# Half a slot later for the values, other places for projections, and SyncE in program order: a change to the attentions of a four-layer kernel

## The chip, the core and the metric

The kernel runs on one core of one Trainium2 chip. The core has five engines that run side by side, each with its own instruction queue: TensorE (PE: matrix products, with the loading of its weights shown as PEld), VectorE (DVE), ScalarE (ACT), GpSimd (POOL) and SyncE (SP), which here only issues transfers. Transfers are carried out by 16 DMA engines. An engine works its queue in order; an instruction that waits holds up everything behind it on its engine.

The metric is the device time of one execution in microseconds, the median of several runs.

## The reference

Four layers follow one another on activations of 8 batches x 256 tokens x 512 features, all in float32: a cross-attention with injected context, a recurrent layer (time mix and channel mix), a transformer decoder block, and a non-local block. The change is in the third, the decoder block, cut here to its attentions:

```python
ln_out = layernorm(hidden_states, ln1_s, ln1_b)
q, k, v = jnp.split(ln_out @ w_qkv + b_qkv, 3, axis=-1)
ctx = merge_heads(attention(split_heads(q), split_heads(k), split_heads(v), ltor_mask))
x = hidden_states + ctx @ w_ao + b_ao

ln_out = layernorm(x, ln2_s, ln2_b)
q = ln_out @ w_q + b_q
k, v = jnp.split(encoder_states @ w_kv + b_kv, 2, axis=-1)
ctx = merge_heads(attention(split_heads(q), split_heads(k), split_heads(v), cross_mask))
x = x + ctx @ w_co + b_co
```

with 16 heads of 32, 256 queries and 256 keys for each batch, and

```python
def attention(q, k, v, mask):
    scores = jnp.einsum('bhqd,bhkd->bhqk', q, k) / jnp.sqrt(jnp.float32(HD))
    scores = scores * mask - 10000.0 * (1.0 - mask)
    probs = jax.nn.softmax(scores, axis=-1)
    return jnp.einsum('bhqk,bhkd->bhqd', probs, v)
```

So there is a self-attention and then a cross-attention, each over 8 batches. The keys and values of the cross-attention come from `encoder_states`, an input of the program.

## The kernel before

One method, `plan`, lays out layer three's attentions together with the recurrent layer before them. The list `runs` has 16 items: the 8 batches of the self-attention (prefix `a_`) and then the 8 of the cross-attention (`c_`). Every item has `CT` = 4 slots, one for each group of 4 heads (128 features), so there are 64 slots, numbered n, which follow the slots of the recurrent layer.

What a slot holds is set in the loop at the end of `plan`. In slot n, in this order:

- `scores(n+1)`: 16 products on TensorE for the next slot's 4 heads (L1127), into PSUM.
- For each of two streams (two heads each): `masked` (VectorE, L1139 and L1142: scale and mask, add, running minimum), `exps` (ScalarE, L1151), `divided` of the stream before (reciprocal on VectorE L1159, products on GpSimd L1161) and `turn` of the stream before that. `turn` transposes 32x32 blocks on VectorE (L1171, `dt`), writes the result to DRAM by a transfer that ScalarE issues (L1175), and reads it back in another order by 4 transfers that SyncE issues (L1177, `pt`). Each of these reads waits for the write, and the write for the transpose. `pt` has two buffers for each of the two streams.
- `fill.until(A0 + n + 0.95)`: the projections and other steps whose place lies in this slot.
- `values(n-1)`: 16 products on TensorE with `pt` of the slot before (L1190), emptied by ScalarE into `cx` (L1194).
- `fill.until(A0 + n + 0.99)`.

The steps that `fill` holds are put in by a table of offsets: a step with offset `at` for item i runs at the place `A0 + CT * i + at`, that is, `at` slots after the item's first slot. The steps of an item are: `at_fetch` (the item's input, `axi`, L1010), `at_inputs` (for the cross-attention the transposed encoder states, `enc`, L1019, one buffer, and the mask `mk`, L1021), `at_norm` and `at_normed` (layer norm, statistics on VectorE; `away` is L1035), `at_norm_T` (transposes on TensorE, L83, emptied by ScalarE), `at_q`, `at_k`, `at_v` (projections, two halves each, L817 and L881, emptied by ScalarE into `aq` L1055, `ak` L1066, `av` L1077), `at_residual` (the input once more, L1084), `at_biased` (GpSimd, L1089), `at_out` (output projection, two halves; its sum is L1095 on VectorE) and `at_store` (L1101). k and v of a cross-attention item read `enc`. Since offsets run from -7.5 to 6.8, the steps of three or four neighbouring items stand in one slot.

Before the change, the TensorE work of the four slots of an item (beside scores and values) is: v1, norm transposes, q1; then q0, out0; then k0, out1; then k1, v0; the values of the slot before stand at each slot's end. Here v1, q1 belong to the item that is running, out0 and out1 to the one before, the rest to the next.

TensorE's instructions keep the order of the program. On the other engines a planner places the instructions by estimated times, save those that are pinned by `pin` (`keep_in_program_order`): the steps of the softmax, the transfers of `turn` and the sums of `at_out` are pinned, the other transfers on SyncE are not. Weights are loaded through `spans`: each weight's entry gives from where to where it is in use, and a load goes out when one of five buffers comes free.

Of the kernel before, what the change touches and what calls it, by code (L numbers as in the profile page):

```python
# [16 lines left out]
P = 128  # L17
B, S, D = 8, 256, 512
# [603 lines left out]
class Middle:  # L622
# [62 lines left out]
    def plan(self):  # L685
        g, cp, wpool = self.g, self.cp, self.wpool
        nc, I = g.nc, g.I
# [19 lines left out]
        def new(tag, bufs=2):  # L707
            return wk.tile([P, CT, S], F32, tag=tag, name=tag, bufs=bufs)
# [4 lines left out]
        def mm(name):  # L713
            return ps.tile([P, 2, S], F32, tag="mm", name=name, bufs=bufs[0])
# [5 lines left out]
        t_ = {}  # L720
# [174 lines left out]
        def spread(b, ct, hf):  # L895

            v_ = t_["v", b]
            vb = vbs[b, ct, hf] = ps.tile([P, NG, 2, S], F32, tag="vb", name="vb", bufs=1)
            for j in range(2):
                for n in range(NG):  # L900
                    r = slice(32 * n, 32 * n + 32)
                    nc.tensor.matmul(  # L902
                        vb[:, n, j, 1:S], lhsT=esel[r, 2 * hf + j, :], rhs=v_[r, ct, 0 : S - 1],
                        start=True, stop=True,
                    )
# [30 lines left out]
        def gather(b, ct, hf):  # L936
            if hf == 0:
                yps[b, ct] = ps.tile([P, S], F32, tag="y", name="yp", bufs=1)
                if ct % 2 == 0:
                    t_["y", b, ct // 2] = wk.tile([P, 2, S], F32, tag="y", name="y", bufs=2)  # L940
            yp = yps[b, ct]
            rs2 = rss.pop((b, ct, hf))
            for j in range(2):
                for n in range(NG):
                    nc.tensor.matmul(
                        yp[32 * n : 32 * n + 32, :], lhsT=gsel[:, 2 * hf + j, :],
                        rhs=rs2[n // 2][:, 2 * (n % 2) + j, :],
                        start=(hf == 0 and j == 0), stop=(hf == 1 and j == 1),
                    )
            if hf == 1:  # L950
                nc.vector.tensor_tensor(
                    t_["y", b, ct // 2][:, ct % 2, :], yp, t_["hv", b][:, ct, :], ALU.add
                )
# [51 lines left out]
        pin = lambda ins: self.tc.keep_in_program_order(ins)  # L1005

        def at_fetch(i):
            pre, b = runs[i]
            x = t_["axi", i] = wk.tile([P, ST, D], F32, tag="xi", name="axi", bufs=1)
            nc.sync.dma_start(out=x, in_={"a_": g.x2, "c_": g.x3, "m_": g.x4}[pre][b])  # L1010

        def at_inputs(i):

            pre, b = runs[i]
            if pre == "a_":
                t_["mk", i], t_["mb", i] = t_["mask"]
                return
            enc = t_["src", i] = wk.tile([P, CT, S], F32, tag="kk", name="enc", bufs=1)
            nc.sync.dma_start(out=enc, in_=I["ctxT"][b].rearrange("(k p) s -> p k s", p=P))  # L1019
            mk = t_["mk", i] = wk.tile([P, ST, S], F32, tag="th", name="mk")  # L1020
            nc.sync.dma_start(out=mk, in_=I["mask_b"][b].rearrange("(t p) k -> p t k", p=P))  # L1021

        def at_mask(i):
            if runs[i][0] == "c_":
# [54 lines left out]
        def at_residual(i):  # L1079
            pre, b = runs[i]  # L1080
            x = t_["axo", i] = new(("hv", "csx")[i % 2], 1).rearrange("p c s -> p (c s)").rearrange(
                "p (t d) -> p t d", t=ST
            )
            nc.sync.dma_start(out=x, in_=(g.x2 if pre == "a_" else g.x3)[b])  # L1084

        def at_biased(i):
            pre, x = runs[i][0], t_["axo", i]
# [9 lines left out]
        def at_store(i):  # L1097
            pre, b = runs[i]
            to = g.x3 if pre == "a_" else g.x4
            to[b] = g.dram([P, ST, D], f"x{pre}{b}")  # L1100
            nc.sync.dma_start(out=to[b], in_=t_.pop(("axo", i)))  # L1101

        def at_load(W, src, col):
            t_[W, 0] = rows_of(g.weight(wpool, I[src], col, W))
# [17 lines left out]
        def scores(i, ct):  # L1122
            sps = t_["sp", i, ct] = [mm("sp") for _ in range(NH)]
            for qt in range(ST):
                for h in range(NH):
                    r = slice(h * HD, (h + 1) * HD)
                    nc.tensor.matmul(  # L1127
                        sps[h][:, qt, :], lhsT=t_["aq", i][r, ct, qt * P : (qt + 1) * P],
                        rhs=t_["ak", i][r, ct, :], start=True, stop=True,
                    )  # L1130
# [48 lines left out]
        def values(i, ct):  # L1179
            pts = [  # L1180
                t_.pop(("pt", i, ct, h2)).rearrange("p r (h t k q) -> p h k t r q", h=2, t=ST, k=ST)
                for h2 in range(2)
            ]
            if ct == 0:
                t_["cx", i] = wk.tile([P, CT, S], F32, tag="g", name="cx")
            cx = mm("cp")[:, 0, :]
            for kt in range(ST):
                for h in range(NH):
                    col = (NH * ct + h) * HD
                    nc.tensor.matmul(  # L1190
                        cx[h * HD : (h + 1) * HD, :], lhsT=t_["av", i][:, kt, col : col + HD],
                        rhs=pts[h // 2][:, h % 2, kt], start=(kt == 0), stop=(kt == ST - 1),
                    )
            nc.scalar.activation(t_["cx", i][:, ct, :], cx, AF.Identity, bias=g.pv(runs[i][0] + "bv", ct))  # L1194
# [31 lines left out]
        fill = self.fill = Filler()  # L1226
# [4 lines left out]
        A0 = 8 * B  # L1231
        for i in range(len(runs)):
            for at, fn, *args in (
                (-7.5, at_fetch), (-5.2, at_norm), (-4.3, at_normed), (-3.5, at_norm_T), (-3.6, at_inputs), (-1.6, at_mask),
                (-2.8, at_q, 0), (-1.8, at_k, 0), (-0.8, at_k, 1), (-0.3, at_v, 0), (0.2, at_v, 1), (0.7, at_q, 1),
                (2.8, at_residual), (4.8, at_biased), (5.7, at_out, 0), (6.7, at_out, 1), (6.8, at_store),
            ):
                fill.put(A0 + CT * i + at, lambda i=i, fn=fn, args=args: fn(i, *args))
        runs.append(("m_", 0))
# [14 lines left out]
        for pre, i, q, kv, o in (("a_", 0, "w_qkv", "w_qkv", "w_ao"), ("c_", B, "w_q", "w_kv", "w_co")):  # L1254
            c = D if q == kv else 0
            for W, lo, hi, src, col in (
                ("wq", -2.8, 0.7, q, 0), ("wk", -1.8, -0.8, kv, c), ("wv", -0.3, 0.2, kv, c + D), ("wo", 5.7, 6.7, o, 0)
            ):
                lo, hi = A0 + CT * i + lo, A0 + CT * (i + B - 1) + hi
                spans.append((lo, hi, lambda W=pre + W, src=src, col=col: at_load(W, src, col)))  # L1260
# [10 lines left out]
        def loop(psums):  # L1271
            every = [(b, ct, hf) for b in range(B) for ct in range(CT) for hf in range(2)]
            bufs[0] = 3
            fill.until(-0.001)
            spread(*every[0])
            for n, at in enumerate(every):
                states(*at)
                fill.until(n + 0.95)
                if n:
                    gather(*every[n - 1])  # L1280
                fill.until(n + 0.99)
                if n + 1 < len(every):
                    spread(*every[n + 1])
            gather(*every[-1])

            psums.close()
            self.ps = psums.enter_context(self.tc.tile_pool(name="atp", bufs=8, space=PSUM))
            bufs[0] = 8
            every = [(i, ct) for i in range(2 * B) for ct in range(CT)]
            stream = [(i, ct, h2) for i, ct in every for h2 in range(2)]  # L1290
            for n in range(-1, len(every)):
                if n + 1 < len(every):
                    scores(*every[n + 1])
                for k in (2 * n + 2, 2 * n + 3):
                    if k < len(stream):
                        masked(*stream[k])
                        exps(*stream[k])
                    if 0 < k <= len(stream):
                        divided(*stream[k - 1])
                    if 1 < k:  # L1300
                        turn(*stream[k - 2])
                fill.until(A0 + n + 0.95)
                if n > 0:
                    values(*every[n - 1])
                fill.until(A0 + n + 0.99)
            values(*every[-1])
            fill.until(999)
            psums.close()
            return t_["ln", 2 * B]
# [455 lines left out]
```

## Time and profile before

| what | us |
|---|---|
| median of 3 runs (lowest, highest) | 3442.02 (3440.96, 3446.04) |
| the profiled execution, its own time | 3442.65 |
| its span in the profile | 3440.9 |
| attention stretch, from the first scores to the start of the next part | 2172 to 2944 |
| start of the scores in first slots of the cross items (the first of them: 2569.25) | 2612.97, 2656.65, 2700.39, 2749.29, 2793.30, 2838.84, 2882.72 |
| of three self items | 2390.43, 2432.61, 2474.19, 2516.66 |

All times are from one execution, recorded by the hardware profiler; the span is the time from the first recorded instruction to the last. A row of the timeline gives the start, the duration, the engine, the line of the kernel, the operation with its output and inputs, the shape, and the number of instructions put together in the row; brackets at its end give the idle time of the engine just before it and what ended that. "ACTq" and "SPq" are the issuing of transfers on ScalarE and SyncE. The granted clock is that of TensorE: 1.0 is full speed.

### The profile page before, as it was taken

The numbers are of one execution on the slowest core, as the hardware profiler recorded it, in microseconds if no ns is written. First come the engines' busy times: TensorE is split into PE (matmuls) and PEld (weight loads), VectorE is DVE, ScalarE is ACT, GpSimd is POOL, SyncE is SP. The second block draws the span as 40 slices with busy tenths as digits, with TensorE's granted clock in tenths as the row PEclk, the third lists the DMA queues.
The fourth block names the chain that finished last, engine by engine and source line by source line (L and its number), as shares of the span: only waits on it lengthen the run. The fifth ranks groups of instructions, "written<-read, shape, count | busy, mean of one in ns | idle before, by whom it ended". The sixth has DMA issues, their size and how long they took to land. (4 is left out here: it accounts for less than half of the span.)

```text
span 3440.9 us, 68745 instructions
## 1 busy us (share of the span) xinstructions
PE 3195.8 (93%) x26496; PEld 2278.9 (66%) x26496; DVE 2407.8 (70%) x4175; ACT 1614.0 (47%) x4000; POOL 1664.5 (48%) x1776
## 2 busy tenths in 40 slices
PE   8999999999999988889999998799989897899999
PEld 6677776777777765656666665465555554689996
DVE  4667666667666663788788788667878777677771
ACT  3455555555555453233443333565656565323223
POOL 6533333333333222555665665343444444688872
PEclk9999999999999998989999999899999999899999
DMA  7666565655656533212233333466677666500002
GB/s 266 218 203 201 188 196 184 206 188 188 214 182 213 178 108 95 96 49 92 94 104 103 105 101 105 139 214 236 237 253 249 238 238 230 182 1 1 1 13 86
DMA packets 277365, 533.08 MB, mean 155 GB/s; under 512 B 25056, under 2 KB 153712, under 8 KB 272944
## 3 DMA queue, kind: packets, MB, share of 16 engines
q1 hardware_dynamic: 255712, 456.48, 41.2%
q10 hardware_dynamic: 20656, 70.39, 5.3%
q8 instruction: 211, 3.46, 0.4%
q0 software_dynamic: 672, 1.81, 0.2%
q14 instruction: 114, 0.93, 0.1%
HBM read 411.15 MB, written 117.44 MB: 154 GB/s over the span
## 5 line engine op out<-in xcount | busy, mean ns | idle before, releaser
L391 POOL TENSOR_SCALAR pe<-pe,rinv 128x512 f32<-128x512 f32 x256 | 177.0, 692 | 614.7 <-DVE rinv L390 604.9
L368 DVE TENSOR_REDUCE nmax<-sp 128x2 f32<-128x1024 f32 x256 | 309.0, 1217 | 183.6 <-PE sp L363 183.6
L933 POOL TENSOR_TENSOR rs<-a,r 128x1024 f32<-128x1024 f32 x128 | 303.1, 2383 | 252.4 <-DVE a L928 215.7
L1161 POOL TENSOR_SCALAR pe<-pe,rinv 128x256 f32<-128x256 f32 x512 | 235.3, 478 | 334.0 <-DVE rinv L1159 316.5
L1151 ACT ACTIVATE pe<-pe,nmax 128x256 f32<-128x256 f32 x512 | 254.6, 498 | 226.1 <-DVE nmax L1142 217.9
L377 ACT ACTIVATE pe<-sp,nmax 128x512 f32<-128x512 f32 x512 | 347.0, 683 | 11.2
L403 DVE STREAM_TRANSPOSE pt<-pe 128x1024 f32<-128x1024 f32 x256 | 312.8, 1231 | 24.2 <-POOL pe L391 15.3
L432 PE MATMUL av<-pt,vr 32*64 32x256 f32 x8192 | 264.6, 388 | 43.6 <-issue 34.9
L928 DVE TENSOR_TENSOR_SCAN a<-w,vb 128x1024 f32<-128x1024 f32 x128 | 287.4, 2276 | 4.8
L432 PEld LDWEIGHTS av<-pt,vr 32*64 32x64 f32 x8192 | 209.8, 135 | 110.8 <-issue 67.3
L363 PE MATMUL sp<-k,q 64*64 64x512 f32 x2048 | 265.8, 611 | 7.3 <-ACT pe L377 7.3
L373 ACT ACTIVATE nmax<-nmax 128x2 f32<-128x2 f32 x256 | 51.8, 202 | 399.9 <-DVE nmax L368 399.7
L303 PEld LDWEIGHTS gp<-t,ws 128*128 128x128 f32 x1512 | 184.8, 192 | 30.5 <-ACT pe L396 11.4
L303 PE MATMUL gp<-t,ws 128*128 128x128 f32 x1512 | 202.2, 277 | 1.8 <-POOL ws L289 1.4
L396 ACT ACTIVATE pe<-pe,rinv 128x512 f32<-128x512 f32 x256 | 182.5, 729 | 41.2 <-DVE rinv L390 41.2
L924 DVE TENSOR_TENSOR vb<-vb,k 128x1020 f32<-128x1020 f32 x128 | 157.2, 1228 | 4.4
L1171 DVE STREAM_TRANSPOSE dt<-pe 128x1024 f32<-128x1024 f32 x128 | 155.6, 1215 | 0.8 <-POOL pe L1161 0.7
L902 PE MATMUL vb<-v,mconstc 32*128 32x255 f32 x1024 | 98.9, 441 | 57.5 <-DVE a L928 57.2
L1443 ACT ACTIVATE h<-h,pvec 128x256 f32<-128x256 f32 x124 | 55.8, 500 | 200.7 <-DVE h L1412 162.5
L1190 PE MATMUL cp<-pt,av 128*32 128x256 f32 x1024 | 97.5, 411 | 55.4 <-DMA pt<-pt 50.1
L390 DVE RECIPROCAL rinv<-ssum 128x2 f32<-128x2 f32 x256 | 41.1, 161 | 146.8 <-ACT pe L377 146.8
L1139 DVE SCALAR_TENSOR_TENSOR sp<-sp,lconstb 128x512 f32<-128x512 f32 x128 | 88.1, 688 | 68.7 <-PE sp L1127 68.6
(310 smaller groups left out, 7623.0 us busy)
## 6 DMA issues: line engine op xcount, KB each, us to landing
pt<-dt ACTq DMA_DIRECT2D x128, 512.0 KB, 3.6
pt<-pt SPq DMA_DIRECT2D x512, 128.0 KB, 3.1
ws<-sqk SPq DMA_DIRECT2D x110, 512.0 KB, 5.0
wqk<-in_wqk_dram SPq DMA_DIRECT2D x70, 512.0 KB, 5.5
vr<-v SPq DMA_DIRECT2D x128, 256.0 KB, 4.7
ws<-sv SPq DMA_DIRECT2D x56, 512.0 KB, 4.8
wv<-in_wv_dram SPq DMA_DIRECT2D x36, 512.0 KB, 4.7
v<-vT SPq DMA_DIRECT2D x64, 256.0 KB, 2.5
```

Of the source, the lines that this page charges most:

```text
L303: nc.tensor.matmul(out[:, hf * P : (hf + 1) * P], lhsT=w[n](hf, k), rhs=a[n](hf, k), start=k == 0, stop=k == ST - 1,)
L363: nc.tensor.matmul(sp[a * 64 : (a + 1) * 64, h, :], lhsT=qs[b, 2 * un + a][r, ic], rhs=ks[b, 2 * un + a][r, :], start=True, stop=True,)
L368: nc.vector.tensor_reduce(nmax, sp, AX.X, ALU.max, negate=True)
L377: nc.scalar.activation(pe[:, h, :], sp[:, h, :], AF.Exp, bias=nmax[:, h : h + 1], scale=1.0 / DH ** 0.5, accum_out=ssum[:, h : h + 1],)
L391: nc.gpsimd.tensor_scalar(pe[:, 0, :], pe[:, 0, :], rinv[:, 0:1], 1.0, ALU.mult, ALU.mult)
L396: nc.scalar.mul(pe[:, 1, :], pe[:, 1, :], rinv[:, 1:2])
L403: nc.vector.transpose(pts[b, un][:, it], pe)
L432: nc.tensor.matmul(av[r][h * DH : (h + 1) * DH], lhsT=vr[rows_, kb, h * DH : (h + 1) * DH], rhs=pt[rows_, :, h, 32 * kb : 32 * kb + 32], s ...
L928: nc.vector.tensor_tensor_scan(a.rearrange("p n l -> p (n l)"), w4.rearrange("p n l -> p (n l)"), vb[:, 4 * n2 : 4 * n2 + 4, :].rearrange( ...
L933: nc.gpsimd.tensor_tensor(rs, a, rb, ALU.mult)
L1151: pin(nc.scalar.activation(pe[:, r, :], pe[:, r, :], AF.Exp, bias=nmax[:, r : r + 1], scale=-1.0, accum_out=ssum[:, r : r + 1],))
L1161: pin(nc.gpsimd.tensor_scalar(pe[:, r, :], pe[:, r, :], rinv[:, r : r + 1], 1.0, ALU.mult, ALU.mult))
```

## The change

Two things change places, and five transfers are pinned:

- `values` stood at the end of slot n and took slot n-1. It now stands in mid slot (after the steps with places below 0.45) and takes slot n-2. After the loop there are therefore two values instead of one.
- The offsets of seven steps change: `at_norm_T` from -3.5 to -3.4, `at_inputs` from -3.6 to -3.45, the first half of k from -1.8 to -2.3, `at_residual` from 2.8 to 3.3, the first half of the output projection from 5.7 to 6.2, `at_store` from 6.8 to 7.3; the spans of the weights of k and out follow. The TensorE work of an item's four slots is then: v1, values, norm transposes, q1; then q0, values, k0; then out0, values, out1; then k1, values, v0.
- SyncE's transfers for `axi`, `enc`, `mk`, the residual and the store are pinned to the order of the program, in which the reads of `turn` already were.

```diff
@@ at_fetch
-            nc.sync.dma_start(out=x, in_={"a_": g.x2, "c_": g.x3, "m_": g.x4}[pre][b])
+            pin(nc.sync.dma_start(out=x, in_={"a_": g.x2, "c_": g.x3, "m_": g.x4}[pre][b]))
@@ at_inputs
-            nc.sync.dma_start(out=enc, in_=I["ctxT"][b].rearrange("(k p) s -> p k s", p=P))
+            pin(nc.sync.dma_start(out=enc, in_=I["ctxT"][b].rearrange("(k p) s -> p k s", p=P)))
             mk = t_["mk", i] = wk.tile([P, ST, S], F32, tag="th", name="mk")
-            nc.sync.dma_start(out=mk, in_=I["mask_b"][b].rearrange("(t p) k -> p t k", p=P))
+            pin(nc.sync.dma_start(out=mk, in_=I["mask_b"][b].rearrange("(t p) k -> p t k", p=P)))
@@ at_residual
-            nc.sync.dma_start(out=x, in_=(g.x2 if pre == "a_" else g.x3)[b])
+            pin(nc.sync.dma_start(out=x, in_=(g.x2 if pre == "a_" else g.x3)[b]))
@@ at_store
-            nc.sync.dma_start(out=to[b], in_=t_.pop(("axo", i)))
+            pin(nc.sync.dma_start(out=to[b], in_=t_.pop(("axo", i))))
@@ the table of steps
-                (-7.5, at_fetch), (-5.2, at_norm), (-4.3, at_normed), (-3.5, at_norm_T), (-3.6, at_inputs), (-1.6, at_mask),
-                (-2.8, at_q, 0), (-1.8, at_k, 0), (-0.8, at_k, 1), (-0.3, at_v, 0), (0.2, at_v, 1), (0.7, at_q, 1),
-                (2.8, at_residual), (4.8, at_biased), (5.7, at_out, 0), (6.7, at_out, 1), (6.8, at_store),
+                (-7.5, at_fetch), (-5.2, at_norm), (-4.3, at_normed), (-3.4, at_norm_T), (-3.45, at_inputs), (-1.6, at_mask),
+                (-2.8, at_q, 0), (-2.3, at_k, 0), (-0.8, at_k, 1), (-0.3, at_v, 0), (0.2, at_v, 1), (0.7, at_q, 1),
+                (3.3, at_residual), (4.8, at_biased), (6.2, at_out, 0), (6.7, at_out, 1), (7.3, at_store),
@@ the spans of the weights
-                ("wq", -2.8, 0.7, q, 0), ("wk", -1.8, -0.8, kv, c), ("wv", -0.3, 0.2, kv, c + D), ("wo", 5.7, 6.7, o, 0)
+                ("wq", -2.8, 0.7, q, 0), ("wk", -2.3, -0.8, kv, c), ("wv", -0.3, 0.2, kv, c + D), ("wo", 6.2, 6.7, o, 0)
@@ the loop
-                fill.until(A0 + n + 0.95)
-                if n > 0:
-                    values(*every[n - 1])
+                fill.until(A0 + n + 0.45)
+                if n > 1:
+                    values(*every[n - 2])
                 fill.until(A0 + n + 0.99)
+            values(*every[-2])
             values(*every[-1])
             fill.until(999)
```

## Prediction, made before the changed kernel had run

> **What bounds the kernel now.** I read the totals, then the attention stretch by windows (where it starts and ends comes from the timeline of its `L1127`), then the list of waits there, then TensorE's and SyncE's timelines through one cross item, and last the places where the clock fell.
>
> ```profile
> PE 3195.8 (93%) x26496; PEld 2278.9 (66%) x26496; DVE 2407.8 (70%) x4175; ACT 1614.0 (47%) x4000; POOL 1664.5 (48%) x1776
> 2172.00:2390.00 218.00, 203.34 (x1066) 124.67 (x1068) 150.06 (x439) 130.98 (x389) 85.97 (x153) 0.95 0.61 211
> 2390.00:2517.00 127.00, 118.96 (x712) 71.94 (x709) 103.98 (x309) 85.05 (x261) 56.64 (x110) 1.00 0.70 239
> 2517.00:2569.00 52.00, 41.43 (x232) 25.29 (x224) 34.47 (x103) 26.79 (x84) 18.05 (x35) 0.93 0.79 273
> 2569.00:2883.00 314.00, 285.57 (x1642) 172.46 (x1636) 241.72 (x717) 196.78 (x600) 134.55 (x258) 0.96 0.69 240
> 2883.00:2944.00 61.00, 40.99 (x184) 18.12 (x182) 30.56 (x85) 21.08 (x68) 19.62 (x36) 0.78 0.72 246
> PE cp L1190 <- DMA pt<-pt: 50.1, 29, 6.9
> PE sp L1127 <- ACT aq L1055: 11.5, 10, 5.3
> DVE sp L1139 <- PE sp L1127: 128.7, 51, 8.7
> DVE away L1035 <- ACT ln_rstd L61: 24.8, 13, 3.3
> ```
>
> A window row gives its length, busy time of TensorE (with TensorE's weight loads next), VectorE, ScalarE and GpSimd, and the granted clock. TensorE sets the end: it is 93% busy, and in the 772 us from 2172 to 2944 it is busy 690.3. What the change can win is the other 81.7 us and the loss of clock. A wait row gives total, times, longest: the largest of TensorE's waits is that of the values for the transposed probabilities, 50.1 us. VectorE waits 128.7 us for scores, since TensorE issues them late.
>
> ```profile
> 2569.25 1.15 PE L1127 MATMUL sp<-ak,aq 32*128 32x256 f32 x16
> 2570.32 3.70 PE L881 MATMUL projs<-c_wv,enc 128*128 128x512 f32 x8
> 2573.86 1.04 PE L83 MATMUL ln_tp<-ident,axn 128*128 128x128 f32 x8
> 2574.73 3.62 PE L817 MATMUL proj<-ln,c_wq 128*128 128x256 f32 x16
> 2578.28 1.60 PE L1190 MATMUL cp<-pt,av 128*32 128x256 f32 x16
> 2580.92 1.15 PE L1127 MATMUL sp<-ak,aq 32*128 32x256 f32 x16 [1.04 <-ACT aq L1055]
> ...
> 2585.88 0.54 SPq L1019 DMA_DIRECT2D enc<-in_ctxT_dram  x1
> ...
> 2713.17 1.92 PE L1190 MATMUL cp<-pt,av 128*32 128x256 f32 x12 [2.96 <-DMA pt<-pt]
> 2715.02 2.09 PE L1127 MATMUL sp<-ak,aq 32*128 32x256 f32 x16
> ```
>
> Each row: start, length, what, and in brackets the idle time before it. T is the start of the scores ahead of v1 (first row). The last two rows show the other cost of a wait: after 2.96 us idle the scores take 2.09 instead of 1.15.
>
> **The change, part by part.** Steps by start-to-start: scores 1.07, v and output projections 3.53, q and k 3.55, norm transposes 0.87, values 1.0. An item is 4 scores, 4 values and 8 projections before and after: no work is added or removed, only order.
>
> *Values later.* Values of slot n-2 stand in mid slot. They need data read some 5 us (half a slot) longer ago, so the 50.1 us of waits should mostly go. Their result feeds only the output projections, which move 0.5 slot too. What the values covered is uncovered: between q1 and the scores that need it, ScalarE must empty q1. Before, these scores start at T+11.67 after values and 1.04 of wait. In the built order of ScalarE the two copies of q1 now stand behind all four norm copies and the probability transfer; I add 0.5 us (one such copy is 0.55). TensorE ends q1 at 1.07+3.53+1.0+0.87+3.55 = T+10.0 and starts scores at T+12.2: 2.2 us idle once per item. Bounds: 1.0 (ScalarE no later) to 4.3 (`aq` at its worst, 5.3, less the values' 1.0).
>
> *k0 earlier, out0 later.* k0 moves from the slot after the next scores to half a slot earlier. In self items its input is the normed tile, made in the slot before. In cross items it is `enc`, a transfer.
>
> *SyncE in order.* Pinned, `enc` goes out behind the 8 reads of its own slot and behind `axi`. It has one buffer, free only when v1 of the previous item has read it (T+4.6), but that is not what ends last: each probability read waits on SyncE for the write before it, which waits for VectorE's transposes (the last of the slot at T+9.4). Before, `enc` also stood behind those reads: issued at T+15.5 to T+17.7 over the items, median 15.7, and k0 could start 5.9 later (2585.88 to 2591.74). Now `axi` (0.5) stands ahead: 15.6 + 0.5 + 5.9 = T+22.0. TensorE asks for k0 at T+12.2 + 1.07 + 3.55 (q0) + 1.0 (values) = T+17.8. New wait: 4.2 us, in each of 7 cross items. Queued behind k0 on TensorE are the next scores, and VectorE waits for those. The residual's load no longer stops SyncE for 39.1 us at the first self item (its longest wait there); The store and the residual go half a slot later: the store's readers are in the next stage, and the residual keeps 1.5 slots (some 15 us) ahead of its bias on GpSimd, against a landing of some 5; nothing. The weights of k and out have their spans moved by half a slot and are loaded once for eight items; nothing. `mk` lands after `enc`, and the masks need it three slots later: nothing.
>
> The clock speaks against trading many small waits for one long one. Rows: half speed after idles of 2.96, 3.23, 4.89 and 6.06 us, 2.2 to 3.0 us lost each time; none after 2.62. [...]
>
> The sum, stretch by stretch:
> - A, 2172 to 2390, first five self items beside the end of the time mix: -6. Gone: the wait for ak of 4.4, pt of 2.8, cn of 2.1 and the half clock behind the first (about 1.9 on scores and k1): 11.2; added 4 exposures of aq at 2.2, less those that run behind other projections: 5. Bounds: -25 (idle 14.7 plus 5% clock of 218 us) and +4.
> - B, 2390 to 2517, three self items of 42.1. VectorE's floor is 34.7 busy + 2.0 for `away` (24.8/13) + 4.0 for scores = 40.7; TensorE's 12.2 + 27.5 = 39.7. 3 x 1.4 = 4.2, of which I take -3. Bounds -7 and 0.
> - C, 2517 to 2569, the first cross inputs: `enc` of that item is issued late whatever the order; k0 at T+26.4, then 21.8 of work and 2.6 of half clock = 50.8 against 52.6: -2. Bounds -6 and +4.
> - D, 2569 to 2883, seven cross items of 44.9. k0 at T+22.0; behind it k0, scores, out0, values, out1, scores, k1, values, v0 = 3.55+1.07+3.53+1.0+3.53+1.07+3.55+1.0+3.53 = 21.8; half clock 2.4. 46.2 per item: 7 x 1.3 = +9. Bounds: +33 (`enc` at T+24.4, the latest issue plus 0.5 + 6.2, and 3.4 of clock: 49.6) and -29 (no wait, VectorE's floor of 40.7).
> - E, 2883 to 2944, tail: 61 us of which TensorE is busy 41.0 at clock 0.78, waiting 4.9, 6.9, 4.1 for pt. Now scores of the last slot no longer stand behind the values that wait 4.9, so VectorE's last transpose comes some 7 us earlier (2922.1 - 2882.7 = 39.4, to about 32); the two last values and outputs follow it unchanged: -9 with the clock they regain. Bounds -12 and -2.
>
> -6 - 3 - 2 + 9 - 9 = -11. Outside 2172 to 2944 nothing moves but the earlier loads of the next stage's weights, off TensorE's path. The profiled execution took 3442.65 (span 3440.9 and 1.75 around it), 0.6 above the median 3442.02: 3442 - 11 = 3431.
>
> **Rivals.**
> - R1, `enc` comes in time. For: SyncE's reads now may run ahead, and a read lands in 3.1. Against: reads wait for writes that follow VectorE, not TensorE. Then cross items go like self items now, 42.1: D = -20, total -40: 3402.
> - R2, slower: `enc`, pinned behind reads, comes at T+24.4, and TensorE stands 6.6 us per cross item and then runs at half clock. For: the reads of an item with a late read put `enc` at T+17.7 already before; scores come 0.5 later and so do reads; the order now may not yield. Against: six of eight items were nearer 15.7. D = +33: +33 - 20 = +13: 3455. It decides from an `enc` ready at about T+23 (46.2 + 1.5 per item cancels the other gains).
> - R3, the waits only move: VectorE's chain, 34.7 us per item plus its stalls for `away` and scores, sets the item, and what pt loses aq gains. For: `aq` now is exposed in every item. Against: VectorE is idle 72 of the 314 us. Then A to D come to nothing and the tail gives 2: 3440.
> - That the change doesn't do what it says: the built order shows all moves; no chance given.
>
> **How the numbers follow.** What a measurement can't tell from no change is 0.2%, 6.9 us: 3435.1 to 3448.9. Forecast 0.45 (own range 3420 to 3444: faster 0.30, same 0.13, slower 0.02); R1 0.17 (faster); R2 0.26 (same 0.02, slower 0.24); R3 0.12 (faster 0.02, same 0.06, slower 0.04). Faster 0.49, same 0.21, slower 0.30. The range goes from R1's to R2's time, 3402 to 3455; half of each lies beyond, about 0.2 in all.
>
> **What would show it.** Waits of the values for pt under 15 us in all; scores after q1 waiting 1 to 3 us for aq in each item; k0 in cross items waiting about 4 us for `enc`, with the scores behind it near 2.09; items in 2569 to 2883 at about 46; the next stage 8 to 10 us sooner after T of the last cross item. Wrong if `enc` waits sum to under 10 us (R1) or over 40 (R2), or if VectorE's idle time in the cross stretch falls below 40 (R3).

## The result, and the profile after

The changed kernel takes 3484.38 us (median of 4, 3477.44 to 3488.63) against 3441.49 (median of 4): a ratio of 1.0123, 95% interval 1.0101 to 1.0146. It is slower by about 42 us, outside the range predicted (3402 to 3455). The profiled execution of it has a span of 3483.3 us, 42.4 more than before.

From the page and the windows of the changed kernel (the same five stretches as before, cut at the starts of the same instructions; length, busy times of PE, PEld, DVE, ACT, POOL, then the granted clock):

```profile
PE 3199.5 (92%) x26496; PEld 2279.9 (65%) x26496; DVE 2410.0 (69%) x4175; ACT 1619.3 (46%) x4006; POOL 1664.6 (48%) x1776
2170.00:2382.00 212.00, 200.68 (x1052) 120.92 (x1052) 150.08 (x445) 134.59 (x391) 85.02 (x151) 0.98 0.63 216
2382.00:2515.00 133.00, 121.28 (x701) 71.45 (x704) 105.40 (x310) 85.52 (x262) 56.95 (x111) 0.97 0.65 225
2515.00:2578.00 63.00, 40.30 (x236) 24.56 (x240) 35.17 (x103) 28.08 (x88) 19.29 (x38) 0.84 0.66 227
2578.00:2926.00 348.00, 288.92 (x1631) 175.52 (x1631) 243.02 (x715) 193.86 (x596) 134.00 (x257) 0.91 0.64 220
2926.00:2987.00 61.00, 42.87 (x205) 18.75 (x203) 31.26 (x86) 21.42 (x71) 19.66 (x36) 0.78 0.72 251
```

Measured more finely, from the first scores, through the scores ahead of v1 in each item, to the start of the next part, the five stretches went from 218.4, 126.2, 52.6, 313.5 and 61.8 us to 211.9, 132.6, 63.0, 348.5 and 60.6: -6.5, +6.4, +10.4, +35.0 and -1.2. The loss is in the cross-attention, and in its clock: 0.91 where it was 0.96.

The list of waits of the changed kernel in this part says for what (total, times, longest):

```profile
DVE sp L1139 <- PE sp L1127: 148.2, 45, 9.6
PE proj L817 <- DMA enc<-in_ctxT_dram: 67.0, 8, 20.9
PE sp L1127 <- ACT aq L1055: 28.4, 16, 5.3
PE cp L1190 <- DMA pt<-pt: 21.4, 10, 7.7
```

The 50.1 us of waits for the probabilities became 21.4, as the change would have it. In their place TensorE waits 67.0 us for `enc`, once per cross item. One of these items, with T = 2679.90, on TensorE and on SyncE of the changed kernel:

```profile
2679.90 1.15 PE L1127 MATMUL sp<-ak,aq 32*128 32x256 f32 x16
...
2686.54 3.62 PE L817 MATMUL proj<-ln,c_wq 128*128 128x256 f32 x16
2692.02 1.15 PE L1127 MATMUL sp<-ak,aq 32*128 32x256 f32 x16 [1.86 <-ACT aq L1055]
2693.10 3.72 PE L817 MATMUL proj<-ln,c_wq 128*128 128x256 f32 x16
2696.75 1.07 PE L1190 MATMUL cp<-pt,av 128*32 128x256 f32 x16
2704.61 5.13 PE L817 MATMUL proj<-enc,c_wk 128*128 128x256 f32 x16 [6.79 <-DMA enc<-in_ctxT_dram]
...
2686.07 1.08 SPq L1101 DMA_DIRECT2D xc<-hv  x1
2687.20 0.48 SPq L1084 DMA_DIRECT2D csx<-xa  x1
2688.85 8.49 SPq L1177 DMA_DIRECT2D pt<-pt  x8
2697.43 0.54 SPq L1010 DMA_DIRECT2D axi<-xa  x1
2698.01 0.46 SPq L1019 DMA_DIRECT2D enc<-in_ctxT_dram  x1
2702.39 0.38 SPq L1021 DMA_DIRECT2D mk<-in_mask_b_dram  x1
```

TensorE is through with the values at T+17.9 and asks for k0; `enc` goes out at T+18.1 and k0 starts at T+24.7, after 6.79 us of idling and at half speed (5.13 us, where k0 at full speed takes 3.6). SyncE had the store and the residual, 1 MB together, right ahead of the eight reads, and `axi` ahead of `enc`. The write that the last four of these reads wait for is issued by ScalarE at 2689.30 (T+9.4) in this item. Its time from issue to landing is in the first row below; the other two are the same write in one item of e5 (T = 2666.58), where store and residual stand elsewhere, and of the kernel before (T = 2656.65):

```profile
DMA to landing us min/median/max: 5.5/5.5/5.5
DMA to landing us min/median/max: 3.4/3.4/3.4
DMA to landing us min/median/max: 3.4/3.4/3.4
```

### The profile page after: what moved, and what is told of

The parts are those of the page before. It is cut to its first block, busy times and chain, and to the rows that moved or that the text cites. A ratio compares the mean times of both kernels' runs of the same rounds, so it can differ in the third digit from the quotient of the medians.

```text
span 3483.3 us, 68747 instructions
## 1 busy us (share of the span) xinstructions
PE 3199.5 (92%) x26496; PEld 2279.9 (65%) x26496; DVE 2410.0 (69%) x4175; ACT 1619.3 (46%) x4006; POOL 1664.6 (48%) x1776
## 5 line engine op out<-in xcount | busy, mean ns | idle before, releaser
L933 POOL TENSOR_TENSOR rs<-a,r 128x1024 f32<-128x1024 f32 x128 | 302.7, 2380 | 251.4 <-DVE a L928 220.6
L432 PEld LDWEIGHTS av<-pt,vr 32*64 32x64 f32 x8192 | 212.3, 137 | 104.8 <-issue 60.5
L1139 DVE SCALAR_TENSOR_TENSOR sp<-sp,mk 128x512 f32<-128x512 f32 x128 | 88.2, 689 | 82.5 <-PE sp L1127 82.5
L817 PE MATMUL proj<-enc,c_wk 128*128 128x256 f32 x256 | 75.9, 462 | 67.0 <-DMA enc<-in_ctxT_dram 67.0
```

What stands on the lines that cost most here:

```text
L432: nc.tensor.matmul(av[r][h * DH : (h + 1) * DH], lhsT=vr[rows_, kb, h * DH : (h + 1) * DH], rhs=pt[rows_, :, h, 32 * kb : 32 * kb + 32], s ...
L933: nc.gpsimd.tensor_tensor(rs, a, rb, ALU.mult)
```

## The experiments

Times are medians of 4 to 12 executions; the ratio is to runs of the kernel before on the same chip, with its 95% interval. Runs on different chips are better compared by their ratios: on the four chips of the experiments the kernel before had medians of 3443.68 to 3448.72 us. The five stretches are those of the one profiled execution of each run, which lies up to 11 us from the median. "`enc` at T+..." is the median over the seven items from the first to the seventh cross item, unless the text says otherwise.

| run | time, us | ratio | five stretches, us |
|---|---|---|---|
| before | 3441.49 | 1 | 218.4, 126.2, 52.6, 313.5, 61.8 |
| the change | 3484.38 | 1.0123 (1.0101 to 1.0146) | 211.9, 132.6, 63.0, 348.5, 60.6 |
| e1 k0, out0 back | 3479.13 | 1.0103 (1.0078 to 1.0128) | 218.8, 129.2, 62.8, 335.8, 61.3 |
| e2 no pins | 3463.44 | 1.0056 (1.0036 to 1.0075) | 212.2, 126.9, 62.2, 334.2, 55.3 |
| e3 values alone | 3460.92 | 1.0053 (1.0035 to 1.0071) | 218.4, 127.9, 56.4, 327.9, 62.1 |
| e4 v1, enc earlier | 3448.57 | 1.0008 (0.9994 to 1.0022) | 213.0, 134.9, 56.0, 310.5, 57.8 |
| e5 store, residual back | 3463.65 | 1.0057 (1.0040 to 1.0074) | 211.9, 125.5, 62.5, 321.7, 63.6 |
| e6 enc by GpSimd | 3432.05 | 0.9966 (0.9953 to 0.9980) | 211.9, 129.4, 57.5, 300.9, 62.4 |
| e7 values alone, enc by GpSimd | 3435.94 | 0.9975 (0.9964 to 0.9986) | 218.0, 128.2, 52.8, 307.5, 61.9 |
| e8 before, enc by GpSimd | 3446.95 | 1.0013 (1.0002 to 1.0024) | 216.5, 129.5, 48.6, 324.7, 56.5 |
| e9 e5 and e6 | 3426.87 | 0.9939 (0.9921 to 0.9956) | 211.9, 125.1, 53.0, 302.4, 62.9 |
| e10 values, pins alone | 3470.32 | 1.0068 (1.0047 to 1.0088) | 218.7, 128.8, 57.6, 332.4, 64.4 |
| e11 e9, other loads by GpSimd | 3500.19 | 1.0154 (1.0134 to 1.0174) | 232.1, 145.7, 59.1, 328.9, 60.5 |
| e12 e6, k0, out0 back | 3442.94 | 0.9989 (0.9976 to 1.0002) | 218.7, 129.9, 56.9, 306.3, 62.1 |
| e13 e10, enc two places forward | 3450.75 | 1.0017 (1.0003 to 1.0030) | 218.4, 128.7, 54.6, 323.9, 63.3 |
| e14 e10, enc three places forward | 3435.25 | 0.9971 (0.9960 to 0.9983) | 218.6, 128.9, 52.6, 305.7, 63.0 |

**e1, e2, e3: undoing one part, or doing one part alone.**

```diff
e1, against the change:
-(-2.3, at_k, 0) ... (6.2, at_out, 0)
+(-1.8, at_k, 0) ... (5.7, at_out, 0)
e2, against the change: the five pin(...) around SyncE's transfers taken off
e3, against before: only the loop's values (slot n-2 at 0.45, two after the loop)
```

> The changed kernel with k0 back at -1.8 and out0 back at 5.7 (their weights' spans too); values, pins and the other places as changed. Theory P (place: k0 asks for enc half a slot before it can be there, and the half clock that follows makes it dearer): the 67 us of enc waits fall under 10, cross items come from 49.8 to 43.5 to 45, time 3425 to 3445. Theory Q (pins: the program's order sends enc late, whoever asks): k0 asks at about T+21.5 and enc lands at T+25 to 27, so 3 to 5 us of wait stay per cross item, 3455 to 3470. Theory V (values later uncover aq and starve VectorE): no more than 10 us come back, 3470 to 3484.

> The changed kernel with the five transfers on SyncE unpinned, all else as changed. P: enc may go out 2 to 4 us sooner, but k0 still asks at T+17.8: 4 us of wait and the half clock stay per item, 3455 to 3475. Q: enc waits fall under 15 us in all, 3430 to 3445. V: 3475 to 3485.

> The kernel before with nothing changed but the values: slot n-2, in mid slot. P and Q: pt waits fall from 50 us to under 20, aq exposed once per item, 3425 to 3442. V: as slow as the change or nearly, 3460 to 3484.

Each gives back part, and no theory fits all three. e1 was to settle it for k0's place and came out at 3479, in theory V's range: with k0 back, `enc` was still late, and later than in the change: issued at T+21 to T+23.5 instead of about T+18. The place of k0 cannot move a transfer in SyncE's pinned order, so something else holds it. e2 came in the time that theory P gave (3463), with 20.7 us of waits for `enc` left in the seven items and 19.2 before the first; but `enc` went out no sooner (T+18.1 against T+18.3), where P had 2 to 4 us. e3, at 3460.92, looked like theory V, the values themselves. But in e3, where the five transfers are not pinned, `enc` went out at a median of T+21.1 as well, against T+15.7 before. What the three have in common is a late `enc`.

**e4: enc earlier, by way of its buffer.**

```diff
e4, against the change (the span of v's weights follows):
-(-3.45, at_inputs) ... (0.2, at_v, 1)
+(-4.1, at_inputs) ... (-0.2, at_v, 1)
```

> The changed kernel with v1 0.4 slot earlier (0.2 to -0.2, so v0 and v1 stand together) and the inputs right behind it (-3.45 to -4.1): enc's one buffer comes free, and its transfer stands, a slot's eight reads earlier in SyncE's order; pins, k0 and values as changed. If enc's lateness at k0 is the whole loss (P and Q together): enc waits under 10 us, 3425 to 3445. If TensorE's wait for enc only stands where VectorE or the transfers would bind anyway: enc waits go, and others take their place, 3465 to 3484.

`enc` now goes out at T+9 to T+13, its waits in the seven items are 6.7 us in all (and 6.7 before the first k0, for which the profile names no releaser), and the cross stretch falls from 348.5 to 310.5, under what it was before. The time, 3448.57, misses the forecast by 4 us. The last three self items are at 134.9 where the change has 132.6, and waits for pt are at 34.0 where it has 21.4; that these are the reason was not tested.

**e5 to e8: what delays enc, and what it costs.**

```diff
e5, against the change:
-(3.3, at_residual) ... (7.3, at_store)
+(2.8, at_residual) ... (6.8, at_store)
e6, against the change (e7: against e3; e8: against before; there without the pin):
-pin(nc.sync.dma_start(out=enc, in_=I["ctxT"][b].rearrange("(k p) s -> p k s", p=P)))
+nc.gpsimd.dma_start(out=enc, in_=I["ctxT"][b].rearrange("(k p) s -> p k s", p=P))
```

> The changed kernel with the residual's load back at 2.8 and the store at 6.8; pins and all other places as changed. Theory S (store and residual, 1 MB, now go out right ahead of the first slot's reads, slow the write those reads wait for and so delay enc by 2 to 3 us): enc issued at T+16 to 17 instead of 18.3, cross items 46 to 47.5 instead of 49.8, 3460 to 3472. Rival (enc is late by its place behind reads and axi alone): enc still at T+18 or later, 3476 to 3488.

> The changed kernel with enc's load issued by GpSimd instead of SyncE, unpinned, all else as changed: enc stands behind no read and behind no completion counter that SyncE and ScalarE share. Theory L (all of the loss is enc reaching k0 late through SyncE's queue, and the clock after it): enc waits under 8 us in all, cross items 43 to 44.5, 3425 to 3442. Rival (once enc is there, aq, pt or VectorE bind in its place): cross items stay over 46.5, 3455 or more.

> The kernel before with the values later (as the run of values alone) and enc's load issued by GpSimd. Theory L: the 14 us that the cross items lost with the values alone (327.9 against 313.5) were enc's place on SyncE: they come back, cross items under 44.9, 3432 to 3446. Rival V (the values' new place itself costs, by aq uncovered for 2 us per item): cross items stay at 46 to 47, 3452 to 3465.

> The kernel before with enc's load issued by GpSimd and nothing else changed. Theory L: enc was just in time, so little is there to win: 3435 to 3446, first cross item 2 to 5 us shorter. Rival (SyncE's queue is shorter by one transfer and reads come sooner): cross items under 43.5, 3425 to 3433.

e5 gave 3463.65, cross items of 46.0 and `enc` at a median of T+17.0 instead of T+18.3: as theory S said. The first read of the first slot's second stream starts at T+13.8 there, in the change at T+15.2, and before at T+13.1, all after a transpose that ends at about T+9.4 (T+10.2 in e5). What differs is the write between the two: from issue to landing it took 5.4 to 6.6 us in the seven items of the change, 3.2 to 3.7 in e5, and before 3.4 to 3.7 in six and 5.6 in the seventh. So the new places of store and residual, which I had costed at nothing, were worth about 20 us by the medians (23 by the ratios); in the profiled executions 27 in the cross stretch and 7 in the last self items, less 3 in the tail.

e6 shows what the loss is. With `enc` sent by GpSimd at T+6, no wait for it is left, and the change is faster than before: 3432.05, the cross stretch 300.9, 47.6 shorter. e7 shows the same for the values alone: 3435.94, so what e3 lost was not the values' new place. e8 shows the other side: before the change, sending `enc` early wins nothing (3446.95, 1 us beyond the forecast), as `enc` was just in time; only the first cross item gets shorter (48.6), and the seven others get longer (324.7), which I have not explained.

**e9, e11, e12: putting it together.**

```diff
e9: e5's and e6's edits together
e11, against e9: axi, mk and the residual also
-pin(nc.sync.dma_start(...))
+nc.gpsimd.dma_start(...)
e12, against e6: e1's edit
```

> The changed kernel with enc's load issued by GpSimd (as e6) and the residual and the store back at 2.8 and 6.8 (as e5). If store and residual also cost by slowing the writes that the reads wait for (theory S): self items 5 to 7 near 125.5 as in e5, cross stretch 293 to 299 where e6 had 300.9, 3418 to 3428. If they hurt only by way of enc: within 4 us of e6, 3428 to 3437.

> As e9, and the loads of axi, mk and the residual are issued by GpSimd too; SyncE keeps the reads of the probabilities and the store. If the reads are held up by the other loads in front of them and their counters: the values' waits for pt fall from 42 us to under 25, 3412 to 3425. If GpSimd's own work (the products of L1161) is held up by issuing: its share rises and scores come later, 3430 to 3445.

> As e6 (enc by GpSimd, store and residual as changed), with k0 and out0 back at -1.8 and 5.7. If the new places of k0 and out0 are worth something once enc is at hand: 5 to 15 us slower than e6, 3437 to 3447. If they are worth nothing by themselves: 3428 to 3436.

e9 beats both kernels: 3426.87, 0.6% under before. Its self items are as short as e5's (125.1), and its cross stretch no shorter than e6's (302.4): in these two profiles, store and residual cost something on their own only in the self items. Its cross window runs at full clock:

```profile
2559.00:2861.00 302.00, 280.88 (x1632) 166.41 (x1632) 238.98 (x709) 194.75 (x592) 137.54 (x260) 1.00 0.75 251
```

e11 was a miss, 55 us beyond its slower forecast. The waits for pt fell as forecast, to 23.7, but VectorE's statistics then stood waiting for `axi`, in their place ahead of the masks. The planner had put them much earlier: in the cross items they wait from T+9.4 on, where in e9 they start at T+31 to T+34, though GpSimd issues `axi` sooner (T+12 to T+13 against T+22 to T+24). So e11 does not price the issuing by GpSimd by itself. The list of waits of e11 (2380 to 2960):

```profile
DVE ln_stats L58 <- DMA axi<-xa: 79.3, 8, 12.4
DVE ln_stats L58 <- DMA axi<-x: 17.8, 2, 9.8
DVE ln_stats L58 <- DMA axi<-xc: 10.3, 1, 10.3
```

e12 is 11 us slower than e6: with `enc` at hand, k0's and out0's new places are worth some 8 to 11 us, most of it in the first self items (211.9 against 218.7).

**e10, e13, e14: why enc is late where the queue ahead of it is the same.** The built program shows something that the kernel's text doesn't: each transfer issued by SyncE or ScalarE signals one of eight counters, taken in turn over both engines in the planner's order, and waits until that counter's last user has landed. A transfer thus waits for the one eight places ahead of it. The traces record these counters as semaphores. In the profiles of before and of the change alike, the 1553 transfers of SyncE and ScalarE use the same eight, and one cycle through the eight fits them from the first to the last; of the 1545 that have an earlier user of their semaphore, none goes out before that one has landed (the closest follows it by 0.016 us). The 13 transfers by GpSimd use eight others. In e1 the one eight places ahead is, for `axi`, the next slot's first probability write, which ScalarE can only issue some 8 us later than the write for the reads before it (five of seven items; 1.7 to 3.9 us of standing). In e3 the last read ahead of `enc` has that place, and stands 3.6 to 4.2 us in every item. e10 was made to have the same order on SyncE as e5 (it has, but for two loads of later weights), and `axi` in that place, which in e5 it isn't; e13 and e14 bring `enc` forward past reads of the first slot's second stream.

```diff
e10: e1's and e5's edits together
e13 (2) and e14 (3), against e10: so many of the four reads of that stream are issued behind enc, and
-(-7.5, at_fetch)
+(-7.4, at_fetch)
```

> The changed kernel with k0 and out0 back at -1.8 and 5.7 and the residual and the store back at 2.8 and 6.8: only the values' place and the pins are left of the change. SyncE's transfers have the same order as in e5. Theory C (the eight completion counters that SyncE's and ScalarE's transfers use in turn: in this build axi, ahead of enc, is eight places behind the next slot's first probability write and must wait for it to land): enc goes out at T+20 to 22 although e5's went out at T+17, k0 waits again, cross items 45.5 to 48, 3460 to 3480. Theory P (k0's place): with k0 back, enc at T+16 to 17 is in time, cross items 43.5 to 45, 3430 to 3445.

> As e10, but in the cross items enc is put two places forward on SyncE: axi goes behind enc and mk, and the last two of the four reads of the first slot's second stream go behind enc. In this build enc itself is now eight places behind the next slot's first probability write. Theory C (counters used in turn): enc, though 1.8 us further forward in the queue, goes out at T+20 to 22 as in e10; 3460 to 3480. Rival (only the queue ahead of it counts): enc at T+14.5 to 16, cross items under 45, 3440 to 3455.

> As e13 with three of the four reads behind enc. enc is now seven places behind that write, and a read, which is not in a hurry, has the eighth. Theory C: enc goes out at T+14 to 16, 5 us or more sooner than in e13 for one place of difference; k0's waits nearly vanish, cross items 43.5 to 45.5, 3440 to 3455. Rival (only the queue counts): 0.6 us sooner than e13, and the same time within 5 us.

Which transfer waits for which one eight places ahead, from the built order and as the semaphores of the traces have it in five to seven of the seven items:

```
e5    axi -> a read of the first slot's first stream;  enc -> the next read;  mk -> the next slot's first write
e10   axi -> the next slot's first write;   enc -> a read
e13   enc -> the next slot's first write
e14   enc -> a read;  the second of the reads behind it is held by the write instead
```

SyncE in one cross item of e5 (T = 2666.58), then SyncE and the issues of the writes on ScalarE in one of e10 (T = 2674.36):

```profile
2666.23 16.72 SPq L1177 DMA_DIRECT2D pt<-pt  x16
2683.04 0.54 SPq L1010 DMA_DIRECT2D axi<-xa  x1
2683.62 0.43 SPq L1019 DMA_DIRECT2D enc<-in_ctxT_dram  x1
```

```profile
2676.31 15.02 SPq L1177 DMA_DIRECT2D pt<-pt  x16
2694.91 0.33 SPq L1010 DMA_DIRECT2D axi<-xa  x1
2695.28 0.43 SPq L1019 DMA_DIRECT2D enc<-in_ctxT_dram  x1
...
2683.75 0.33 ACTq L1175 DMA_DIRECT2D pt<-dt  x1
2691.83 0.33 ACTq L1175 DMA_DIRECT2D pt<-dt  x1
```

In e5 `axi` follows the last read at once. In e10 SyncE is through with the reads at 2691.33 and then stands 3.6 us, until 3.1 us after the write at 2691.83, which landed at 2694.85. `enc` goes out at T+20.9 and not at T+17.0; 3470.32 us, as theory C said. Theory P, which had `enc` out at T+16 to T+17, is out for this run; that k0 in its old place finds such an `enc` nearly in time is what e14 then shows. e5 itself has one item in which the turn of the counters puts `enc` behind that write (T = 2615.84): there it stands 4.9 us behind an `axi` that has long been issued, and goes out at T+21.4.

e13 (T = 2620.29) and e14 (T = 2607.29), SyncE and the next slot's first write on ScalarE:

```profile
2626.73 12.05 SPq L1179 DMA_DIRECT2D pt<-pt  x14
2642.30 0.39 SPq L1019 DMA_DIRECT2D enc<-in_ctxT_dram  x1
...
2638.54 0.33 ACTq L1177 DMA_DIRECT2D pt<-dt  x1
```

```profile
2611.53 12.78 SPq L1179 DMA_DIRECT2D pt<-pt  x13
2624.35 0.59 SPq L1019 DMA_DIRECT2D enc<-in_ctxT_dram  x1
2624.99 6.92 SPq L1179 DMA_DIRECT2D pt<-pt  x3
...
2624.76 0.33 ACTq L1177 DMA_DIRECT2D pt<-dt  x1
```

In e13 `enc` waits 3.5 us behind reads that are done, for the write at 2638.54 to land. In e14, one place further on, it goes out before the write is even issued, and the stop moves to the reads behind it (6.92 us for three, which take 1.9 unhindered). Over the items `enc` goes out at a median of T+21.7 in e13 and T+17.2 in e14: 4.5 us for one place, where the queue alone would give 0.6. e14's T+17 is later than the T+14 to T+16 forecast, as the reads ahead of `enc` were. Both times came out below theory C's forecasts, by 9 and 5 us, and e13's lies in the rival's; it is the issue of `enc` and not the total that tells the two apart. What made e13 faster than e10, with `enc` no sooner, was not tested, but part of it is in the traces: in e13, with no load ahead of it, `enc` lands 3.9 to 4.0 us after its issue in four of the seven items, and in e10, behind `axi`, 5.3 to 5.4 us in four; k0 idles 5.3 us in the seven items and not 21.8. The waits on SyncE say the same of the counters (2570 to 2930, e13; e14 has no such row for `enc`):

```profile
SPq L1019 <- DMA pt<-dt: 23.2, 6, 5.1
```

## Why the prediction was wrong

- *Right: what is exposed and when TensorE asks.* Scores after q1 wait 1.86 us where I had 2.2; k0 is asked for at T+17.9 in four of the seven cross items, where I had T+17.8, and at T+19.6 in the other three; the wait of the values for pt shrank, though to 21.4 and not under 15. Stretch A gave -6.5 for -6.
- *Right in mechanism: enc, and the clock behind it.* I had named the wait for `enc`, in that place, and the half-speed stretch that follows it. The sum has no lost clock for the 2.2 us of idling for `aq`; that held in four of the seven cross items only: in the other three a stretch of 3.41 us at half speed begins 1.2 to 1.5 us behind it (at 2591.5, 2741.7 and 2840.6), and the first of these made q0 5.41 us long instead of 3.7. That cost little, as k0 then waits for `enc` in any case. The reading "none after 2.62" was wrong already for the kernel before, where half speed starts at 2688.65 and 2825.18, with waits of 1.53 and 1.63 us and a shorter one just ahead. What the profiles show of the clock beside this is in the last section.
- *The step that failed: "15.6 + 0.5 + 5.9 = T+22.0".* Its first term is the end of the reads as the kernel before had it. In the change the reads ended at T+17.8 (median), so `enc` went out at T+18.3, and k0 started 6.5 and not 5.9 us behind it, at T+24.8. The last term was read from an `enc` with no load ahead of it; behind `axi` it took 6.3 us to land (median) where before it took 4.9. With the 21.8 us of work, T+24.8 leaves 3.2 us for lost clock and small waits to the 49.8 measured per item. That is the upper bound of stretch D, T+24.4 and 49.6 us: D gave +35.0, which I had as R2's price of +33. No run shows the 3.4 us of clock in that bound: in the change the half-speed stretches behind the waits for `enc` cost 1.46 to 2.85 us per item, as half of TensorE's busy time in them. R2's T+24.4 came from the latest issue before, T+17.7, in the one item whose write took 5.6 us with neither store nor residual beside it (why, no run shows); that it came so near is luck.
- *The edit costed at nothing: store and residual.* I looked at who waits for them, not at what they stand ahead of. Moved half a slot they go out right before the reads of a slot, with 1 MB, and the write these reads wait for lands some 2 us later (T+15.1 instead of T+13.0). This is what moved the 15.6. e5, which takes the two moves back, has k0 at T+22.5 and 46.0 us per item, so there the sum for D (T+22.0 and 46.2) holds. e5 puts the two moves at about 20 us, and with the moves taken back B is 125.5 where the change has 132.6: they are why it went up by 6.4 instead of down by 3.
- *Stretch C, "issued late whatever the order".* The first `enc` went out at T+34.8 instead of T+21.1: pinned behind the loads of `c_wv` and `axi`, and then 7.3 us more by a counter (`axi` at 2541.97, `enc` at 2549.65), whose last user in the built order is the next slot's second write, issued at 2542.48. TensorE stood 20.9 us: +10.4 where I had -2; e9 has 53.0. The T+26.4 that I summed with had no row behind it: before, the first k0 started at T+30.3, 9.2 us behind its `enc`.
- *Stretch E.* -1.2 where I had -9: VectorE's last transpose came 3.7 us sooner after T and not 7, and the last read 1.6, so the two last values still wait for pt (7.7 us the longest).
- *What was not on my list.* The counters. They decide in e1, e3 and e10 when `enc` goes out, and made undoing the place of k0 (e1) look nearly useless; e14, with k0 undone too and `enc` at T+17.2, has next to no waits for it. In the change itself they hold the first `enc`, and from then on mostly `mk` behind it (15.1 us in five waits of SyncE); in one item only, T = 2628.11, do they stop a read ahead of `enc` (4.7 us) and `enc` (0.8).

R2 had the price of D right, and not the rest: it took the other stretches as in the forecast, -20, where they gave +9. R1 came true in e6 and e9, with `enc` in time by another way; the gain was 12 us in e6 and 21 in e9 by their ratios, and not 40: waits for pt were 34.3 us again in e9, and those for `aq` 27.1.

## What to carry to other kernels

When a consumer is moved ahead, look up when its input can be there in the new order, and price the case in which it comes as late as the profile shows anywhere, not the median alone: here that was the difference between a forecast of a gain and one of a loss. A load or store whose own reader has time can still have a price, by the transfers that it goes out just in front of: here about 20 us (e5). And where a transfer sits idle behind transfers that are done, look in the built order for the one whose completion it shares a counter with: here one place of shift brought the issue of `enc` forward by 4.5 us (e13, e14). A load with no producer (`enc`) did better here when GpSimd issued it, at T+6 to T+9 (e6 to e9) where the change had T+18.3, while the same done to three more loads (e11) cost 73 us against e9, with their consumers in other places by the planner.

## What the runs showed of the hardware and the program that was not expected

- SyncE's and ScalarE's transfers in this program hold up one another across engines by the eight counters: stops of 3 to 5 us per item on SyncE with nothing due in front of them (e10, e13), gone for `enc` with one place of shift (e14). Transfers by GpSimd are not among these eight: `enc` then goes out at T+6 to T+9 (e6 to e9).
- A probability write of 512 KB took 3.4 to 3.7 us from issue to landing in six of the seven cross items before, and 5.4 to 6.6 us in the change, with a store and a load of 512 KB each issued 1.3 to 3.5 us before it.
- All stretches at half clock in the change's attention last 3.41 us or a multiple of it. The idles of 5.15 to 9.46 us for `enc` in the seven items each left k0 at 5.1 to 6.5 us instead of 3.6. Waits of 1.86 us for `aq` were followed by half speed in three of seven items and in four not.
- In the profile of the change the three differ from the four in how busy TensorE was in one window of 3.41 us. In it and in the one of before, all half-speed stretches (41 and 36) start on one grid of 3.4133 us, to within 1 ns, and the wait of 1.86 us falls on it differently. In two windows of that grid in the change with such a wait, each shown with the window behind it (length, busy PE, PEld, DVE, ACT, POOL, granted clock), TensorE was busy 1.54 and 1.86 us:

```profile
2588.07:2591.48 3.41, 1.54 (x19) 1.16 (x19) 0.37 (x1) 2.19 (x6) 0.03 (x1) 1.00 0.93 342
2591.48:2594.89 3.41, 3.41 (x10) 2.70 (x9) 3.34 (x12) 2.18 (x8) 3.12 (x4) 0.50 0.45 157
2690.47:2693.88 3.41, 1.86 (x20) 1.43 (x21) 0.69 (x1) 1.86 (x5) 0.64 (x1) 1.00 1.02 382
2693.88:2697.29 3.41, 3.41 (x26) 2.62 (x28) 3.34 (x13) 2.19 (x8) 2.84 (x5) 1.00 0.36 110
```

The other two items that lost clock had 1.55 us in the window of the wait; the other three that did not had 1.68 in one, or the wait spread over two windows of 2.4 to 2.6. In the two profiled executions of before and of the change, cut on that grid by their records of the clock and of TensorE's instructions, all 49 full-clock windows with TensorE busy for under 40% were followed by half clock, 24 of 63 with 40 to 62%, and 2 of 1763 with over 62%. Beyond these counts no run shows what sets the clock.
